# Transposes and gates of later tokens moved from the first attention steps into the opening maxima of a fused attention and mixture-of-experts block

## The chip, the core and the metric

The kernel runs on one core of a Trainium2 chip. The metric is device time in microseconds (us) of one execution; lower is better. The five queues that matter are named as in the profile: PE (TensorE, matrix products and transposes; PEld is its weight load), DVE (VectorE), ACT (ScalarE), POOL (GpSimd) and SP (SyncE, which issues most of the DMAs).

## What is computed

The input is x of shape 4 x 1024 x 256 (four sequences of 1024 tokens). All matrices are float32.

```python
xn = layernorm(x)                                   # over the 256 channels
x  = x + attention(xn) + moe(xn)
# attention: 16 heads of 16, rotary embedding, softmax(q k^T / 4) v, output projection
# moe: scores = sigmoid(xn @ w_gate.T), 16 experts in 4 groups, best 2 groups, best 4 experts,
#      routed SwiGLU experts (hidden 128) weighted by the scores, plus a shared SwiGLU (hidden 256)
```

## The kernel before

**Tokens.** There are 4096 tokens. The class `Norm` handles them in eight blocks of 512, numbered q = 0 to 7; blocks 2b and 2b+1 are sequence b. Four things are done to a block. `scale(q)` (L453) normalises it in place on ACT, four instructions of 128x256 with the factors `rstd` and `off`; these factors come from POOL (`power`, L371, L372, L409, L410 for blocks 2 to 4, L414, L416, L418 for 5 to 7). `turn(q, pair)` (L482, L486) transposes half a block: four transposes on PE into one bank of PSUM, and a copy by ACT into `part[q]`. `store(q)` writes the normalised rows to DRAM (`xnd`), and for blocks from 4 on the transposed part is written to `xnTd`. `gate(qs)` (L499, L508) multiplies the transposed parts with the gate weights, and `logits_of(qs)` (L515, L522) turns the products back and copies them to `logits`, from which the routing starts in step 9.

**Opening.** Blocks 0 and 1 (the first sequence) are normalised and turned first. A loop over ten values of t then makes q, k and v of sequence 0: products on PE (L1149), rotary embedding on DVE or POOL (`rotate`, L1180 to L1189), transposes back (`turn_unit`, L1216) and copies by ACT into `qT` and `kT` (L1221). The statistics of the later blocks run beside that, on DVE for blocks 2 to 4 and on ACT for 5 to 7 (L390, L396). In the same loop the first maxima are taken: `max_round(b, g, s)` makes four products `pm` (L1235), each 128x512, which DVE reduces to row maxima (L1243). A round with even s needs only the first half of `kT`, one with odd s the second half, and so the last copy of `kT`. After the loop come the factors of blocks 2 to 7 on POOL (issued after the last `rotate`), `scale(2)`, four rounds with odd s (16 products and 16 reductions), and `max_off` (L1254, L1258, L1263), which subtracts the maxima from q.

**Steps.** The attention then runs in 256 steps. A step makes four products `ps` (L1277) with four exponentials by ACT (L1286), four products `pm` with four maxima for the next head group, and four products `av` (L1302) of an earlier step's exponentials, whole (512 columns) or in two halves of 256. Steps 0 to 6 carry an additional round of maxima each (step 6 carries two). `moves(step)` issues scalings and stores, `pieces(step)` returns units that PE does in the middle of the step: turns, gates and logits of the blocks among them.

**What sets the order.** PE's instructions stay in the order of the text, and so do the copies of `turn_unit` for sequence 0, the statistics on ACT, the factors on POOL and `scale(q)` for q under 4. All other instructions are placed by the compiler's scheduler, which decides the order of each engine's queue by its own estimates; `issue_after` sets a lower bound for one group. All products share eight banks of PSUM in rotation, so a product waits until the reader of the bank eight places before it is done.

Of the kernel before, what the change touches and what calls it, by code (L numbers as in the profile page):

```python
# [20 lines left out]
NT = B * TT  # L21
# [7 lines left out]
HALF = 512  # L29
QT = 4  # L30
# [21 lines left out]
def kernel(  # L52
# [30 lines left out]
    k = Kit(tc, banks)  # L83
# [38 lines left out]
    norm = Norm(k, att, ff, keep, logits, power)  # L122
# [44 lines left out]
    with tc.issue_after(k.rotary):  # L167
        for power_of in powers:
            power_of()
    norm.scale(2)  # L170
    for qt in range(4):
        att.max_round(0, 0, 2 * qt + 1)
    att.max_off(0, 0, 0)

    def weights():
        nc.scalar.dma_start(out=k.w1s_sb, in_=w1s.rearrange("(c p) f -> p c f", p=P))
        nc.scalar.dma_start(out=k.w3s_sb, in_=w3s.rearrange("(c p) f -> p c f", p=P))
        nc.scalar.dma_start(out=k.w2s_sb, in_=w2s.rearrange("(c p) h -> p c h", p=P))
        k.sp(wout_sb, w_out.rearrange("(c p) f -> p c f", p=P))
# [81 lines left out]

    ex = ExitStack()
    now = pieces(0)
    for step in range(STEPS):
        beside.tick()
        norm.moves(step)
        if step in k.at_step:
            with tc.issue_after(k.last_exp):
                k.at_step[step]()

        bits = []
        if routing is not None and step >= ROUTE_FROM:
            bits += [advance] * (1 if step >= PUT_FROM else 2 if k.ranking else 3)
        if step >= PUT_FROM and beside.put_next < n_put:
            assert k.slots_known
            bits[:0] = [beside.put] * 2
        if step > done.get("tiles", STEPS):
            if beside.got == 0:
                ex.close()
                beside.rows = att.rows = ctx.enter_context(  # L280
                    tc.tile_pool(name="gp", bufs=4, side="right")
                )
            for _ in range(2 if step < STEPS - 2 * TT else 1):
                bits += [beside.get, beside.add]
        then = pieces(step + 1) if step + 1 < STEPS else []

        att.step(now, bool(then) and (step + 1 > 6 or step + 1 in norm.gates), bits)
        now = then
# [4 lines left out]
class Kit:  # L293


    def __init__(self, tc, banks):
        self.tc, self.nc, self.banks = tc, tc.nc, banks
        self.last_sp = self.last_exp = None
        self.ranking = self.slots_known = False
        self.summed = self.shared_rows = 0  # L300
# [26 lines left out]
class Norm:  # L327
# [3 lines left out]
    def __init__(self, k, att, ff, keep, logits, power):  # L331
        self.k, self.nc, self.att, self.ff = k, k.nc, att, ff
        self.logits, self.power = logits, power
        self.gates = {3: (2, 3, 4, 5), 5: (6, 7)}
        self.less = keep.tile([P, NT], F32, name="less")
        self.sq = keep.tile([P, NT], F32, name="sq")
        self.x4, self.xnT, self.part, self.lg = {}, {}, {}, {}
        self.mv, self.rstd, self.off, self.scaled = {}, {}, {}, None
# [28 lines left out]
    def power_of(self, q):  # L367
        nc, ff, mv = self.nc, self.ff, self.mv[q]
        rstd = self.rstd[q] = ff.tile([P, QT], F32, name=f"rstd_{q}", tag="rstd", bufs=8)
        keep = self.k.tc.keep_in_program_order  # L370
        keep(nc.gpsimd.tensor_scalar_add(mv[:, :, 1], mv[:, :, 1], 1e-5))  # L371
        keep(nc.gpsimd.tensor_tensor(rstd, mv[:, :, 1], self.power, ALU.pow))  # L372
# [155 lines left out]
    def moves(self, step):  # L528

        k = self.k  # L530
        q = step + 3
        if q < NT // QT:
            with k.tc.issue_after(k.last_exp or k.pace):
                self.scale(q)
        if step + 2 < NT // QT:
            self.store(step + 2)
        if 4 <= step + 1 < NT // QT:
            b, hf = divmod(step + 1, 2)
            k.sp(k.xnTd[b][:, :, hf * HALF : (hf + 1) * HALF], self.part[step + 1])

    def pieces(self, step, own):
        out = []
        if step + 2 < NT // QT:
            out += [lambda: self.turn(step + 2, 0), lambda: self.turn(step + 2, 1)]
        if own:
            out.append(own.pop(0))
        if step in self.gates:
            out.append(lambda: self.gate(self.gates[step]))
        if step - 1 in self.gates:
            out.append(lambda: self.logits_of(self.gates[step - 1]))  # L550
        return out + own
# [1002 lines left out]
```

## Time and profile before

| | |
|---|---|
| device time, median of 3 runs | 1416.7 us (1416.4 to 1418.83) |
| the profiled execution: device time | 1417.86 us |
| its span in the profile | 1416.2 us |
| PE, DVE, ACT, POOL busy | 98%, 66%, 55%, 30% of the span |
| mean granted PE clock | 0.993 |

The span is the time from the first to the last instruction that the profile shows; 1.66 us of the device time lie around it. The profiled execution took 1.16 us more than the median. PE's busy time is modelled from pipelined instructions, so a high share does not mean that it runs at its peak.

### The profile page before, as it was taken

The page shows a single profiled execution, that of the slowest core. Times are in us where ns is not written, and L with a number is a line of the kernel's source. Part 1 is how long each engine was busy: PE and PEld are TensorE (multiplying, and loading weights), DVE is VectorE, ACT ScalarE, POOL GpSimd, SP SyncE. Part 2 cuts the span into 40 slices and gives each one's busy share as a digit, 9 for nine tenths or more (in the row PEclk, how much of TensorE's full clock was granted, in tenths as well). Part 3 has the DMA queues.
Part 4 walks back from the last instruction along what each step waited for, and adds up shares of the span by engine and source line. Part 5 has one row for each costly group of instructions (what it writes and reads, how often), then busy time and mean ns, then how long its engine had stood idle before and what let it go on. Part 6 is the DMA issues. An engine that isn't in the chain of part 4 may idle for free.

```text
span 1416.2 us, 25822 instructions
## 1 busy us (share of the span) xinstructions
PE 1390.9 (98%) x9438; PEld 656.3 (46%) x9438; DVE 929.1 (66%) x1734; ACT 783.6 (55%) x1586; POOL 424.1 (30%) x498
## 2 busy tenths in 40 slices
PE   7899999999999999999999999999999999999998
PEld 4443233443343335666566665565664343333333
DVE  6879758678777765445554555554447988999941
ACT  4565445555555555556555555555555555555575
POOL 5401503764444464220000000002224444445400
PEclk9899999999999999999999999999999999999999
DMA  6134752424232314556666666665432434433310
GB/s 187 58 129 168 262 180 63 153 75 137 91 112 100 106 60 157 171 165 219 209 213 191 211 201 209 201 193 180 149 120 68 122 106 132 127 109 113 108 39 31
DMA packets 136670, 199.10 MB, mean 141 GB/s; under 512 B 13920, under 2 KB 99040, under 8 KB 136288
## 3 DMA queue, kind: packets, MB, share of 16 engines
q1 hardware_dynamic: 103088, 137.78, 30.6%
q0 software_dynamic: 12288, 33.57, 7.6%
q10 hardware_dynamic: 21168, 26.10, 5.4%
q8 instruction: 75, 1.23, 0.4%
q14 instruction: 51, 0.42, 0.1%
HBM read 124.01 MB, written 79.69 MB: 144 GB/s over the span
## 4 chain that ended last, share of the span: by engine, by line
PE 96%; DVE 2%; DMA 1%; ACT 1%; issue 0%; POOL 0%; ACTq 0%; POOLq 0%; DVEq 0%
PE ps L1277 20%; PE pm L1235 20%; PE av L1302 18%; PE ph_r L823 9%; PE exy L982 5%; PE ph_s L855 4%; PE pqk L1149 4%; PE py L1371 2%; PE pso L892 2%; PE pv L1149 2%; PE ext L973 2%; PE ptr L1216 2%; PE pmt L1258 1%; PE po L1326 1%; DVE mx L1243 1%; PE pt L482 1%
## 5 line engine op out<-in xcount | busy, mean ns | idle before, releaser
L1286 ACT ACTIVATE es<-ps 128x512 f32<-128x512 f32 x1024 | 554.8, 596 | 460.9 <-PE ps L1277 238.5
L1243 DVE TENSOR_REDUCE mx<-pm 128x1 f32<-128x512 f32 x1024 | 660.9, 685 | 188.4 <-PE pm L1235 138.5
L1277 PE MATMUL ps<-q,kT 32*128 32x512 f32 x1792 | 510.3, 643 | 4.2 <-DVE mx L1243 3.3
L1235 PE MATMUL pm<-kT,qT 32*128 32x512 f32 x1792 | 511.7, 643 | 1.4 <-ACT kT L1221 1.4
L1302 PE MATMUL av<-es,vv 128*32 128x512 f32 (+1 forms) x2136 | 277.4, 590 | 0.0
L1277 PEld LDWEIGHTS ps<-q,kT 32*128 32x128 f32 x1792 | 143.5, 183 | 193.7 <-ACT es L1286 140.0
L1235 PEld LDWEIGHTS pm<-kT,qT 32*128 32x128 f32 x1792 | 147.6, 183 | 64.7 <-DVE mx L1243 26.8
L831 DVE SCALAR_TENSOR_TENSOR th_r<-th_r,ph_r 128x256 f32<-128x256 f32 x72 | 30.3, 421 | 199.6 <-ACT th_r L830 199.6
L938 POOL DMA_INDIRECT xs<-rows,slot_i x128 | 124.0, 969 | 121.8 <-DVE mx L1243 107.7
L1030 POOL DMA_INDIRECT yg<-ys,slot_i x128 | 121.8, 951 | 119.1 <-DVE mx L1243 111.2
L1180 POOL TENSOR_TENSOR rot<-qk,sin_sb 128x256 f32<-128x256 f32 x56 | 39.5, 728 | 392.2 <-DVE qk L1137 392.0
L823 PE MATMUL ph_r<-xT,w 128*128 128x128 f32 x1152 | 140.5, 275 | 0.5 <-ACT xT L976 0.5
L1302 PEld LDWEIGHTS av<-es,vv 128*32 128x32 f32 x2136 | 42.9, 108 | 199.6 <-issue 177.7
L823 PEld LDWEIGHTS ph_r<-xT,w 128*128 128x128 f32 x1152 | 134.4, 192 | 0.8 <-ACT xT L976 0.7
L982 PE MATMUL exy<-w,gu_r 128*128 128x256 f32 x288 | 76.6, 388 | 0.0
L1277 PE MATMUL ps<-q,qkT 32*128 32x512 f32 x256 | 74.3, 640 | 0.0
L1235 PE MATMUL pm<-qkT,qkT 32*128 32x512 f32 x256 | 73.4, 640 | 0.0
L830 ACT ACTIVATE th_r<-ph_r 128x256 f32<-128x256 f32 x72 | 27.7, 384 | 82.6 <-PE ph_r L823 82.6
L982 PEld LDWEIGHTS exy<-w,gu_r 128*128 128x128 f32 x288 | 50.6, 190 | 28.9 <-issue 21.7
L1047 DVE SCALAR_TENSOR_TENSOR sum<-yg,wk,sum 128x256 f32<-128x256 f32 x128 | 63.7, 498 | 0.3 <-DMA yg<-ys,slot_i 0.3
L988 ACT ACTIVATE y<-exy 128x512 f32<-128x512 f32 x72 | 43.2, 600 | 35.0 <-PE exy L982 29.9
L1116 POOL MEMSET vv<- 128x128 f32 x4 | 1.3, 318 | 142.7 <-ACT es L1286 142.7
(178 smaller groups left out, 1230.0 us busy)
## 6 DMA issues: line engine op xcount, KB each, us to landing
w<-we SPq DMA_DIRECT2D x144, 384.0 KB, 4.0
xs<-zero ACTq DMA_DIRECT2D x8, 2304.0 KB, 8.1
xg<-xs SPq DMA_DIRECT2D x72, 256.0 KB, 4.7
ys<-y SPq DMA_DIRECT2D x72, 256.0 KB, 4.7
acc<-acc SPq DMA_DIRECT2D x14, 512.0 KB, 4.2
xb<-in_x_dram SPq DMA_DIRECT2D x16, 256.0 KB, 3.1
acc<-xb SPq DMA_DIRECT2D x16, 256.0 KB, 2.8
rows<-xnd SPq DMA_DIRECT2D x8, 512.0 KB, 5.8
```

The lines of the kernel that those rows point to most:

```text
L823: nc.tensor.matmul(ph[:, n, at], lhsT=w[n][:, c, :], rhs=xT[:, c, at], start=(c == 0), stop=(c == NC_ - 1),)
L855: nc.tensor.matmul(ph, lhsT=w[:, i, c * P : (c + 1) * P], rhs=self.xnT[b][:, i, at : at + SL], start=(i == 0), stop=(i == NC_ - 1),)
L938: put = nc.gpsimd.indirect_dma_start(out=k.xs, out_offset=bass.IndirectOffsetOnAxis(ap=k.slot_i[:, t, kk : kk + 1], axis=0), in_=self.rows ...
L982: nc.tensor.matmul(py[:, r, :], lhsT=gus[i][:, r * P : (r + 1) * P], rhs=got[i][1][:, r, 2 * NC_ * F :], start=True, stop=True,)
L1030: get = nc.gpsimd.indirect_dma_start(out=self.yg[:, kk, :], out_offset=None, in_=k.ys, in_offset=bass.IndirectOffsetOnAxis(ap=k.slot_i[:, ...
L1047: nc.vector.scalar_tensor_tensor(sm[:, 0, :], yg[:, kk, :], k.wk[:, t, kk : kk + 1], sm[:, 0, :], ALU.mult, ALU.add)
L1149: nc.tensor.matmul(ps, lhsT=self.xnT[b][:, c, t * P : (t + 1) * P], rhs=self.wqkv_sb[:, c, at : at + w], start=(c == 0), stop=(c == NC_ - 1),)
L1235: nc.tensor.matmul(ps, lhsT=self.qT[b, g // 2][rows, g % 2, qt * P : (qt + 1) * P], rhs=self.kT[b, g // 2][rows, g % 2, hf * HALF : (hf + ...
L1243: k.pace = nc.vector.tensor_reduce(out=self.mx_of[b, g, qt // 4][hf][:, qt % 4, j, :], in_=ps, axis=AX.X, op=ALU.max,).ins
L1277: nc.tensor.matmul(ps, lhsT=self.kT[b, g // 2][rows, g % 2, kc * P : (kc + 1) * P], rhs=self.q2[b, g, qh][rows, :], start=True, stop=True,)
L1286: k.last_exp = nc.scalar.activation(e, ps, AF.Exp, scale=DH**-0.5).ins
L1302: nc.tensor.matmul(av[32 * j : 32 * j + 32, cols], lhsT=self.vv[b][:, kc, h * VS : h * VS + 32], rhs=es[j][:, cols], start=(kc == 0), stop ...
```

## The change

Blocks 2 to 5 (the second and third sequence) are scaled and turned before step 0, between and after the four odd rounds of maxima, where before only block 2 was scaled. `scale(3)` follows `scale(2)`; the two turns of block 2 stand behind the second and third of these rounds, those of blocks 3 and 4 behind the fourth, those of block 5 behind `max_off`. `scale(4)` stands behind the second round, `scale(5)` ahead of `max_off`. In the steps, only blocks 6 and 7 are still scaled (in steps 0 and 1, before in steps 3 and 4) and turned (in steps 2 and 3, before 4 and 5). The gates of blocks 2 to 5 move from step 3 to step 1, those of 6 and 7 from step 5 to step 4; the logits follow a step later, as before. The writes of the transposed parts to `xnTd` are rearranged to fit. A step whose successor has a gate does its `av` product whole, so the steps that do this move as well.

```diff
@@ tile_block_kernel
     norm.scale(2)
+    norm.scale(3)
+
     for qt in range(4):
         att.max_round(0, 0, 2 * qt + 1)
+        if qt == 1:
+            norm.turn(2, 0)
+            norm.scale(4)
+        if qt == 2:
+            norm.turn(2, 1)
+    for q in (3, 4):
+        for pair in range(2):
+            norm.turn(q, pair)
+    norm.scale(5)
     att.max_off(0, 0, 0)
+    for pair in range(2):
+        norm.turn(5, pair)
@@ Norm.__init__
-        self.gates = {3: (2, 3, 4, 5), 5: (6, 7)}
+        self.turns, self.gates = {2: 6, 3: 7}, {1: (2, 3, 4, 5), 4: (6, 7)}
@@ Norm.moves
-        q = step + 3
+        q = step + 6
         if q < NT // QT:
             with k.tc.issue_after(k.last_exp or k.pace):
                 self.scale(q)
         if step + 2 < NT // QT:
             self.store(step + 2)
-        if 4 <= step + 1 < NT // QT:
-            b, hf = divmod(step + 1, 2)
-            k.sp(k.xnTd[b][:, :, hf * HALF : (hf + 1) * HALF], self.part[step + 1])
+        q = step + 4 if step < 2 else self.turns.get(step - 1)
+        if q:
+            b, hf = divmod(q, 2)
+            k.sp(k.xnTd[b][:, :, hf * HALF : (hf + 1) * HALF], self.part[q])
@@ Norm.pieces
-        if step + 2 < NT // QT:
-            out += [lambda: self.turn(step + 2, 0), lambda: self.turn(step + 2, 1)]
+        if step in self.turns:
+            out += [lambda i=i: self.turn(self.turns[step], i) for i in range(2)]
```

## Prediction

> **What bounds the kernel now.** The page says that the whole is a matter of PE: the chain that ended last lies on it for 96% of the span. That is an average, so I read next the same chain in order of time for the stretch that the change touches, from 43 us to 70 us.
>
> ```profile
> PE 96%; DVE 2%; DMA 1%; ACT 1%; issue 0%; POOL 0%; ACTq 0%; POOLq 0%; DVEq 0%
> ```
>
> ```profile
> 47.64 0.44 ACT kT L1221
> ...
> 48.12 1.18 PE pm L1235 x8
> 49.30 9.65 DVE mx L1243 x16
> ...
> 59.22 1.13 PE pmt L1258 x4
> ...
> 60.44 0.70 DVE q L1263
> ...
> 61.19 1.21 PE ps L1277
> ```
>
> (start, length, what.) The opening is a relay: ACT's last copy into kT lets the odd rounds start at 48.12, DVE then reduces 16 products in 9.65 us while PE has little to do, and the first product of step 0 comes at 61.19. Whoever delays that copy delays all of it. From 61.19 on the chain is PE's, with each turn as a link (`PE pt`, 1.66 us in step 0, 1.02 to 1.03 us in steps 1 to 5).
>
> The second view is the timeline, of ACT and then of POOL, just before these rounds.
>
> ```profile
> 45.09 0.64 ACT L1221 COPY qT<-ptr 128x256 f32<-128x256 f32 x2
> ...
> 47.64 0.70 ACT L1221 COPY kT<-ptr 128x256 f32<-128x256 f32 x2
> 48.17 4.14 ACT L453 ACTIVATE qkT<-qkT,off,rstd 128x256 f32<-128x256 f32 x8
> ```
>
> ```profile
> 47.26 0.23 POOL L410 TENSOR_SCALAR off<-off 128x4 f32<-128x4 f32 x1
> ...
> 49.97 0.23 POOL L410 TENSOR_SCALAR off<-off 128x4 f32<-128x4 f32 x1
> ...
> 52.51 0.24 POOL L410 TENSOR_SCALAR off<-off 128x4 f32<-128x4 f32 x1
> ...
> 54.46 0.20 POOL L418 TENSOR_TENSOR off<-less,rstd 128x4 f32<-128x4 f32 x1
> ```
>
> ACT scales only after its last copy, at 48.17. POOL finishes the factors of blocks 2, 3, 4 and 5 at 47.49, 50.20, 52.75 and 54.66, one behind the other, with no gap that something could fill.
>
> The third view is the busy time by stage: steps 0 to 6, cut at each step's first `ps`.
>
> ```profile
> 61.20:67.90 6.70, 6.70 (x35) 3.48 (x36) 3.16 (x6) 3.21 (x7) 0.00 (x0) 0.75 0.00 0
> 67.90:74.60 6.70, 6.70 (x39) 2.81 (x37) 5.80 (x11) 5.45 (x12) 0.00 (x0) 1.00 0.63 196
> ...
> 103.00:110.90 7.90, 7.90 (x59) 3.31 (x55) 7.47 (x15) 2.86 (x6) 0.00 (x0) 1.00 0.02 9
> ```
>
> (Window, length, busy PE, PEld, DVE, ACT, POOL, granted PE clock, DMA.) Step 6, with twelve maxima and no turn, keeps DVE busy 7.47 of 7.90 us, while steps 0 to 5, with eight maxima, last 6.4 to 7.65 us.
>
> **Part 1: the turns leave the steps.** Blocks 2 to 5 are four turns of eight transposes. Of the six steps with a turn, four lose theirs: 1.66 us (the one in step 0, at a clock of about half) and 3 x 1.03 us, 4.75 us of links on the path. Is there room? A step without turn would be 6.4 - 1.03 = 5.4 us, above its eight reductions (8 x 0.61 = 4.9 us), so DVE does not take the gain away at once. Three scalings (2.06 us of ACT each, blocks 4 to 6) leave the steps too; they delay exponentials (the first of step 2 starts at 76.20, as the scaling from 74.24 ends), but no link of the chain is ACT's there. I take 0, bounds 0 and 1.0 us. One more `av` is split, two halves of 0.57 us for one whole of 1.00: +0.14. The gates and logits cost PE the same in their new steps. Sum -4.6 us, bounds -6.0 (scalings count, step 0 gets the full clock) and -3.0 (DVE's idle pieces around its eight reductions come back in part).
>
> **Part 2: the turns in the opening.** The transposes of blocks 2 to 4 stand among 16 products that DVE takes 0.60 us each to reduce; six groups of four (1.03 / 2, or 1.66 / 2 at half clock) are 3.1 to 5 us beside 9.65 us. The banks suffice: a turn's bank is wanted again eight allocations later, some 4.8 us of reductions. I cost them at 0; if the cover were gone, it is those 3.1 to 5 us. Block 5 is different: its eight transposes stand between `pmt` and the first `ps`. Before, `pmt` to `ps` is 1.97 us (59.22 to 61.19), at a clock of half. PE now needs 1.12 + 1.73 = 2.85 us there at half clock (+0.88), or 0.66 (the `pmt` at 112.43) + 1.09 = 1.75 us at full, when DVE's part is also shorter (-0.4). I take +0.4 and keep both ends.
>
> **Part 3: what the moved scalings do to ACT's queue.** This decides the sign. `scale(4)` and `scale(5)` are not held in the order of the text, and the order of the changed program's instructions on ACT shows where the scheduler put them:
>
> ```
> ... 6 squares of blocks 6 and 7 (L396)
> scale(4) x2                     waits for off of block 4 (POOL)
> qT, qT, kT, kT of token tile 6
> 2 squares of block 7
> scale(4) x2, scale(5) x3        waits for off of block 5 (POOL)
> qT, qT, kT, kT of token tile 7  <- the copy that the odd rounds need
> scale(2) x4, scale(3) x4, scale(5) x1, scale(6) x4, then the copies of the turns
> ```
>
> Up to the first of these lines all queues stand as before, and POOL's whole order is unchanged. So ACT comes to `scale(4)` at 45.09, where it copied qT before, and the factors come at 52.75: a wait of 7.66 us. Queued behind it are the eight copies of tiles 6 and 7, for which PE waits, and for PE DVE. To this come seven scalings ahead of the last kT copy, at 4.14 / 8 = 0.52 us each: 3.6 us. The odd rounds start at 48.12 + 11.3 = 59.4 instead of 48.12. `off` of block 5 (54.66) is there before ACT gets to it (about 56.9). POOL does not wait for anything behind the stall before block 7's factors, so there is no second stall.
>
> [...]
>
> Then the clock. PE has no instruction from 46.75 to 59.4. Before, the granted clock was 0.50 from 54.65 to about 64.8, after a stretch with thinly spread products. So I start the rounds at half clock: the first reduction came 1.16 us after its product at 48.12, but 2.15 us after the one at 61.19, at half: +1.0 us (bounds +0.2 and +1.0). Sixteen reductions at 0.60 us are slower than PE at either clock.
>
> [...]
>
> **The sum.** Stall and scalings +11.3, cold first products +1.0, block 5 ahead of `ps` +0.4: step 0 begins at about 73.9 instead of 61.19. Steps -4.6. Together +8.1 us. Nothing after step 6 is changed, and PE bounds it, so the delay stays. The profiled execution (span 1416.2, 1.66 around it) becomes 1417.86 + 8.1 = 1426.0; the median of the runs lies 1.16 us below that execution, so I say 1424.8. Bounds: 11.0 + 0.2 - 0.4 - 6.0 = +4.8 (1421.5) and 11.6 + 1.0 + 0.9 - 3.0 = +10.5 (1427.2).
>
> **Rivals.** (1) The turns' gain does not come: DVE paces steps 0 to 5 at what they cost now, and the steps give back 1 us only. For it: DVE is busy 5.80 of 6.70 us in step 1. Against: in step 2 it idles 1.08 us exactly during the turn. Then +11.7, 1428.4; chance 0.12. (2) The change does what its text says: ACT isn't held up. That needs block 4's `off` ready at 45.1 rather than 52.75, or copies that run past the waiting scaling. Then -4.6, with part 2 hidden: 1412.1. It decides from the point where stall and scalings together are under about 3 us. Against it: POOL's rotation ends only at 45.15, and the factors follow it in order. Chance 0.06. (3) The delay is made up: scalings and half clock were dearer in the steps than I count, and 8 to 10 us come back. Then within 0.2%: 1418; chance 0.05. My forecast keeps 0.77.
>
> About 0.2% (2.8 us) is what a measurement of this kernel can tell from no change. Slower by more: 0.77 + 0.12 = 0.89; within: 0.05; faster: 0.06. The range, 1421.0 to 1428.5, takes in the bounds and rival 1.
>
> **What would show it.** In the changed profile ACT should idle some 7.7 us before its first L453, released by POOL; the odd `pm` should start near 59.4, `pmt` near 71.5, the first `ps` near 73.9; steps 0 to 6 should take about 45 us instead of 49.7. I am wrong if ACT shows no such wait, if `pm` starts before 55, or if the steps are not shorter.

## The result and the profile after

The changed kernel takes 1420.9 us (median of 12 runs, 1419.68 to 1422.58) against 1416.89 us for the kernel before (12 runs, 1415.1 to 1419.21): ratio 1.0027, 95% interval 1.0019 to 1.0034, or 2.7 to 4.8 us slower. The forecast was 1424.8 us with a range from 1421.0 to 1428.5: the sign was right, the size (+8.1 us) was twice what was measured (+4.0), and the median lies 0.1 us below the range.

The chain of waits of the profile after (start, length, what) has a new beginning: it no longer comes to the odd maxima by ACT's copies alone but by POOL's factors.

```profile
52.14 0.25 POOL off L424
...
52.41 1.09 ACT qkT L467 x2
...
55.56 2.45 ACT qkT L467 x5
...
58.53 0.28 ACT kT L1236
...
58.85 2.12 PE pm L1250 x8
60.98 9.65 DVE mx L1258 x16
...
70.90 0.66 PE pmt L1273 x4
71.55 0.87 PE pt L496 x8
72.43 0.67 PE ps L1292
```

(Line numbers are larger by 14 or 15 than before.) The odd products start at 58.85 instead of 48.12. The timeline of ACT and of PE gives the two waits, in square brackets (the idle time before the row, and what ended it):

```profile
52.41 1.09 ACT L467 ACTIVATE qkT<-qkT,off,rstd 128x256 f32<-128x256 f32 x2 [7.51 <-POOL off L424]
58.85 3.79 PE L1250 MATMUL pm<-kT,qT 32*128 32x512 f32 x16 [12.41 <-ACT kT L1236]
```

ACT idles 7.51 us for block 4's factor, and PE, whose kT copy stands behind it, 12.41 us. The busy time by stage, of steps 0, 1 and 6 (columns as in the prediction):

```profile
72.40:76.70 4.30, 4.30 (x29) 2.45 (x28) 3.10 (x6) 2.98 (x7) 0.00 (x0) 1.00 1.01 322
76.70:83.60 6.90, 6.90 (x50) 2.16 (x48) 6.36 (x11) 4.59 (x9) 0.00 (x0) 1.00 0.87 288
...
108.30:115.90 7.60, 7.60 (x55) 3.38 (x51) 7.17 (x14) 2.95 (x6) 0.00 (x0) 1.00 0.00 1
sum 43.50, PE 43.50 PEld 18.00 DVE 36.56 ACT 21.40 POOL 0.95; mean PE 6.21 PEld 2.57 DVE 5.22 ACT 3.06 POOL 0.14
```

Steps 0 to 6 take 43.5 us instead of 49.7; step 0 shrank most, from 6.70 to 4.30 us, and its granted clock is 1.00 instead of 0.75. The cut between steps 0 and 1 lies at the second product `ps` of step 1, about 1.1 us late, here and in the profile before, where the prediction calls it the first; from first product to first product step 0 went from 5.58 to 3.14 us, which is the same 2.4 us less.

In what follows four places serve as marks: the start of the odd products, the first reduction of them, the first `ps`, and the `pmt` of step 7. Between the two profiles the change has cost 5.0 us at that `pmt` (117.46 against 112.43), but only 2.6 us at the end of the span (1418.8 against 1416.2). Where the rest went is a question for the experiments.

### The profile page after: what moved, and what is told of

The parts are those of the page before. It is cut to its first block, busy times and chain, and to the rows that moved or that the text cites. A ratio compares the mean times of both kernels' runs of the same rounds, so it can differ in the third digit from the quotient of the medians.

```text
span 1418.8 us, 25831 instructions
## 1 busy us (share of the span) xinstructions
PE 1385.4 (98%) x9446; PEld 655.4 (46%) x9446; DVE 929.6 (66%) x1734; ACT 784.3 (55%) x1586; POOL 424.4 (30%) x498
## 4 chain that ended last, share of the span: by engine, by line
PE 95%; DVE 2%; POOL 1%; DMA 1%; ACT 1%; issue 0%; ACTq 0%; POOLq 0%; DVEq 0%
PE ps L1292 20%; PE pm L1250 20%; PE av L1317 18%; PE ph_r L838 9%; PE exy L997 5%; PE ph_s L870 4%; PE pqk L1164 4%; PE py L1386 2%; PE pso L907 2%; PE ext L988 2%; PE pv L1164 2%; PE ptr L1231 2%; PE pmt L1273 1%; PE po L1341 1%; DVE mx L1258 1%; PE pf L1374 1%
```

## The experiments

Ratios are to the kernel before on the same chip and in the same session, with 95% intervals. The places come from each kernel's one profile, in us; starting points differ by up to 1 us between profiles of the same kernel, so the differences in the second and third column say more than the first.

| kernel | odd products start | first reduction to first `ps` | first `ps` to `pmt` of step 7 | ratio |
|---|---|---|---|---|
| before | 48.12 | 11.91 | 51.24 | |
| before_again | 49.11 | 11.89 | 51.65 | |
| changed | 58.85 | 11.44 | 45.06 | 1.0027 (1.0019 to 1.0034) |
| after_again | 59.03 | 11.44 | 45.04 | 1.0043 (1.0029 to 1.0057) |
| order_kept | 48.46 | 11.70 | 45.05 | 0.9959 (0.9943 to 0.9975) |
| scalings_only | 59.91 | 11.90 | 51.03 | 1.0060 (1.0047 to 1.0073) |
| scalings_kept | 48.72 | 11.90 | 50.12 | 0.9989 (0.9979 to 0.9998) |
| dose | 61.42 | 11.70 | 45.05 | 1.0039 (1.0024 to 1.0053) |
| gates_late | 48.04 | 11.70 | 45.31 | 0.9954 (0.9940 to 0.9967) |
| six_too | 48.56 | 11.69 | 45.05 | 0.9946 (0.9932 to 0.9959) |
| filler | 49.42 | 11.44 | 49.65 | 0.9986 (0.9975 to 0.9997) |

**order_kept: the change without the stall.** The scheduler may no longer place the scalings of blocks 4 to 6 ahead of the last copies into kT.

```diff
 # Norm.scale, changed kernel
-            if q < 4:
+            if q < 7:
                 self.k.tc.keep_in_program_order(scale)
```

> The changed kernel, but the scalings of blocks 4, 5 and 6 are held in the order of the text, so that none of them stands ahead of the last copies into kT. Theory A (ScalarE's wait for the factors of block 4 and seven scalings ahead of the last copy cost the opening some 11 us; the turns taken out of the steps bring about 6 us): the odd maxima start near 48.1 us again, the first ps near 61 us, and steps 0 to 6 stay as short as in the changed kernel (45.1 us from the first ps to the pmt of step 7): pmt near 106.5 us, device time 5 to 7 us under the kernel before, about 1411. Rival B (the turns themselves hold up the opening, since PE and the banks are not free beside the maxima): first ps not before 64 us, device time at or above that of the kernel before.

The odd products start at 48.46, the first `ps` at 61.32, `pmt` at 106.37, and the kernel is 3.6 to 8.1 us faster than before (0.25% to 0.57% of 1423.63 us in that session). Theory A is right in every place, and rival B is out: with the transposes among the odd maxima, first reduction to first `ps` is 11.70 us against 11.91, so they cost the opening nothing. The chain that leads to its first exponential runs over the products and turns, and at its end over ACT's scaling of block 6, which led to six_too below:

```profile
48.46 2.00 PE pm L1250 x16
50.46 0.59 PE pt L496 x4
51.04 2.83 PE pm L1250 x8
53.87 0.59 PE pt L496 x4
54.46 1.80 PE pm L1250 x8
...
62.01 0.57 ACT x L467 x2
...
63.98 0.49 ACT es L1301
```

**scalings_only: the stall without the turns.** The kernel before with the scalings in their new places.

```diff
 # kernel before
     norm.scale(2)
+    norm.scale(3)
     for qt in range(4):
         att.max_round(0, 0, 2 * qt + 1)
+        if qt == 1:
+            norm.scale(4)
+    norm.scale(5)
     att.max_off(0, 0, 0)
 # Norm.moves
-        q = step + 3
+        q = step + 6
```

> The kernel before, with only the scalings moved as in the change (blocks 3, 4 and 5 ahead of step 0, block 6 in step 0, block 7 in step 1); turns, gates and writes stay in their old steps. Theory A: the stall of the changed kernel is here too (odd maxima near 58.9 us, first ps near 72.4 to 73), but not the gain: steps 0 to 6 take about 49 to 51 us to the pmt of step 7 as before, and device time is 10 to 12 us above the kernel before (1427 to 1429). Rival C (the 6 us gained in the steps come from the scalings that left them, not from the turns): steps as short as in the changed kernel, about 45 us, and device time about 4 to 5 us above the kernel before.

The stall is there (ACT idles 7.52 us, odd products at 59.91) and the steps stay at 51.03 us. So theory A holds for both places, and rival C, by which all the gain comes from the scalings, is out. That a part of it does come from them, the next kernel shows; in scalings_only TensorE was at half clock (0.50) from 73.9 to 79.0, over 5 us of step 0 where it was 3.4 us in the kernel before (0.50 from 61.2 to 64.6), which hides some of what the scalings gave back. The device time rose less than expected, 6.7 to 10.4 us instead of 10 to 12. The profiled execution, 1434.21 us, was the longest of five (median 1431.4); where the rest went is not shown.

**scalings_kept: the scalings moved, without stall.** This is scalings_only with `q < 7` in the condition of order_kept.

> As scalings_only, with the scalings of blocks 4, 5 and 6 held in the order of the text, behind the last copies into kT: no stall. Theory A: the opening is as before (odd maxima near 48.1 us, first ps near 61.2), the steps too, device time within 1.5 us of the kernel before. Rival C (the scalings made the steps long): pmt of step 7 near 107 us rather than 112, device time about 5 us under the kernel before.

It is 0.3 to 3.0 us faster, and the steps are 1.1 us shorter than the first profile of before (50.12 against 51.24; 1.5 against the second). Theory A's "as before" is a little off: scalings in the steps were not quite free.

**dose: another wait, other work.** This is the changed kernel with `q < 6` in that condition, so block 6's scalings are placed early instead of block 4's.

> The changed kernel with the scalings of blocks 4 and 5 held in the order of the text, but not that of block 6: the scheduler then puts two scalings of block 6 where two of block 4 stood, and two more ahead of the copies of token tile 7, so that ScalarE waits for factors that come about 3.7 us later, with four scalings ahead of the last copy instead of seven. Theory A: ScalarE idles about 11.2 us instead of 7.5 and the odd maxima start near 61.0 us, 2.2 us later than in the changed kernel; device time about 2 us above it (1423). A theory in which the place of the scalings matters by the work they add (rival D): start near 57.3 us, 1.5 us earlier, and 1419.

```profile
56.44 1.09 ACT L467 ACTIVATE x<-x,off,rstd 128x256 f32<-128x256 f32 x2 [11.03 <-POOL off L432]
```

ACT idles 11.03 us and the odd products start at 61.42, 2.57 us later than in the changed kernel (0.5 us of it because this profile is later as a whole: POOL's factors began at 45.44 instead of 44.94). Four scalings instead of seven stand ahead of the copy, and it is still later: rival D, by which the added work alone decides, is out. Both count: the wait is 3.5 us longer, the three scalings fewer save about 1.5. Device time, 3.4 to 7.5 us above before, fits theory A but is too wide to show 2 us.

**gates_late: of the turns and gates, only the turns of blocks 2 to 5 moved.**

```diff
 # Norm.__init__, on top of order_kept
-        self.turns, self.gates = {2: 6, 3: 7}, {1: (2, 3, 4, 5), 4: (6, 7)}
+        self.turns, self.gates = {4: 6, 5: 7}, {3: (2, 3, 4, 5), 5: (6, 7)}
```

> As order_kept (the change without the stall), but the turns of blocks 6 and 7 and all gates stay in the steps of the kernel before (turns in 4 and 5, gates in 3 and 5): only the turns of blocks 2 to 5 are moved. Theory A: the sooner gates bring nothing, since the routing starts in step 9 in any case: first ps to the pmt of step 7 within 0.5 us of order_kept's 45.05 us, device time within 2 us of order_kept. Rival E (sooner gates are worth something): 1 us or more longer to the pmt, or a longer stretch behind it.

It takes 45.31 us in the steps against 45.05, and its ratio is order_kept's, as far as two intervals of some 4 us width from two sessions can tell. The sooner gates bring nothing that these runs can measure.

**six_too: block 6 scaled in the opening too.**

```diff
 # on top of order_kept
     norm.scale(5)
+    norm.scale(6)
     att.max_off(0, 0, 0)
 # Norm.moves
-        if q < NT // QT:
+        if step and q < NT // QT:
```

> As order_kept, but block 6 is scaled with block 5 ahead of the last maximum instead of between the last turns and the first exponentials (all scalings held in the order of the text, block 7 in step 1). Theory A: the first exponential of step 0 starts about 2 us sooner than in order_kept (63.98 us there); since the maxima on VectorE pace step 0, this brings 0 to 1 us, device time 0 to 1 us under order_kept and 6 to 8 us under the kernel before. A rival in which the exponentials pace step 0: 2 us under order_kept.

It is 5.8 to 9.7 us faster than before (0.9932 to 0.9959 of 1420.79 us), but its 45.05 us to the `pmt` are order_kept's. What it was made for did not come: the first exponential starts at 63.79 instead of 63.89, not 2 us sooner. In both kernels ACT is busy without a gap from block 5's scaling (58.90 and 58.80) to that exponential, with block 6's scaling and the two copies of block 5's last turns in between; only the order of these two changed. So this run does not decide whether the exponentials pace step 0, and whether it is better than order_kept the two intervals don't tell.

**filler: the clock alone.** Twenty-four transposes that nobody reads, at the places of the moved turns of blocks 2 to 4.

```diff
 # kernel before
+    def filler(n):
+        pt = k.bank([P, 4, P], f"fill_{n}")
+        for i in range(4):
+            k.pe(nc.tensor.transpose(pt[:, i, :], k.ident, k.ident))
+
     for qt in range(4):
         att.max_round(0, 0, 2 * qt + 1)
+        if qt in (1, 2):
+            filler(qt)
+    for n in range(4):
+        filler(4 + n)
     att.max_off(0, 0, 0)
```

> The kernel before, with 24 additional transposes of the identity at the places where the changed kernel has those of blocks 2 to 4 (four behind the second and third odd round, sixteen behind the fourth); nobody reads them, and nothing else is moved. Theory A (the transposes among the odd maxima keep TensorE's clock open, whatever they are good for, and that is part of the gain): no half clock between 50 and 66 us; first reduction of the odd rounds to first ps about 11.5 us instead of 11.9, first ps to the pmt of step 7 about 50.3 us instead of 51.2 to 51.65 (step 0 no longer cold); device time 1 to 1.5 us under the kernel before. Rival F (the clock closes because the rounds are thin, and 24 transposes do not change that, so that in the changed kernel the clock opened for another reason): half clock at 55 to 65 us as before, 11.9 and 51.2 us, device time unchanged.

Busy time and granted clock (the number before the last two) of the odd maxima, first of the kernel before, then of filler:

```profile
49.28:54.65 5.37, 5.37 (x23) 2.49 (x19) 5.37 (x9) 3.03 (x7) 4.99 (x31) 0.97 0.55 183
54.65:61.19 6.54, 2.68 (x8) 0.72 (x5) 5.17 (x10) 0.00 (x0) 2.81 (x7) 0.50 0.17 52
```

```profile
50.58:54.65 4.07, 4.07 (x20) 1.60 (x14) 4.07 (x7) 3.02 (x7) 3.69 (x29) 1.00 0.40 138
54.65:62.00 7.35, 5.13 (x33) 3.31 (x32) 6.46 (x12) 0.00 (x0) 4.08 (x10) 1.00 0.35 104
```

The clock stays at 1.00 where it was 0.50. First reduction to first `ps` falls to 11.44 us, as in the changed kernel, the steps to 49.65 (50.3 was expected), and the kernel gets faster by 0.4 to 3.6 us for work that is of no use. Theory A is right and rival F is out: the transposes among the odd maxima hold the clock open, and that is a gain of its own, some 0.5 us in the opening and 1.6 us in step 0 (2.0 against the second profile of before).

**after_again and before_again: the stretch behind step 7.** Both kernels unchanged, for a second profile.

> The changed kernel unchanged, for a second profile and beside the other kernels on one chip. Theory A (everything behind step 7 costs the same in both kernels, apart from how long TensorE's clock happens to be halved between 130 and 220 us): 3 to 6 us above the kernel before; odd maxima near 58.9, first ps near 72.4, pmt of step 7 near 117.5 us; the stretch from the first to the third reciprocal of the attention (81.3 us in the first profile) between 80.5 and 84.5 us, longer with more time at half clock. Rival E (the sooner gates shorten that stretch for good): again 81.3 us or less, and the kernel before again 84.5.

> The kernel before unchanged, for a second profile. Theory A: first to pmt of step 7 as in the first profile (first ps to that pmt 51.2 us), but the stretch from the first to the third reciprocal of the attention between 81 and 84.5 us with less than 10.2 us at half clock. Rival E: 84.5 us again.

The changed kernel is 4.1 to 8.1 us slower than before here (3 to 6 were expected). From the `pmt` of step 7 to the first reciprocal of the attention (L1331 before) it is 19.25 or 19.26 us in all eleven profiles, whatever the kernel. From there to the third reciprocal the length differs, and for the most part it goes with the clock. The rows of this stretch in the first profiles of before and changed, then in the second ones:

```profile
131.70:216.20 84.50, 81.20 (x467) 29.49 (x468) 57.69 (x107) 39.04 (x73) 23.40 (x33) 0.94 0.60 214
```

```profile
136.70:218.00 81.30, 78.42 (x468) 29.48 (x468) 57.77 (x108) 39.07 (x73) 23.37 (x33) 0.98 0.63 223
```

```profile
133.07:214.70 81.63, 79.20 (x468) 29.15 (x468) 55.98 (x108) 39.04 (x73) 24.05 (x33) 0.96 0.62 222
```

```profile
136.88:219.60 82.72, 79.38 (x468) 29.25 (x468) 57.67 (x107) 39.03 (x73) 23.38 (x33) 0.96 0.61 219
```

A mean of 0.94, 0.96 and 0.98 means about 10, 6.5 and 3.3 us at half clock (an estimate: the share that is missing, twice, by the length; the clock records of the first profiles of before and changed hold 1.00 and 0.50 only, with 10.2 and 3.4 us at 0.50 in these rows). Over all eleven profiles the stretch took 80.7 and 81.3 us at 0.98, 81.6 to 83.4 us at 0.96 (seven profiles), and 84.5 and 84.6 us at 0.94; the 1.9 us within the middle group are not explained by it. The kernel before was once in the longest group and once in the middle one; six_too, a fast kernel, was in the longest. Rival E, 3 us for good from the sooner gates, is out: the stretch varies by that much from run to run of one kernel. A small effect is not: the five profiles with the sooner gates average 82.2 us, the six others 83.0, and each set spreads over 3 to 4 us. The first pair of profiles happened to draw 3.3 us in favour of the changed kernel, and 0.9 us came back behind the third reciprocal; this is how 5.0 us at step 7 became 2.6 us at the end. In the second pair 3.81 us at the `pmt` (117.62 against 113.81) became 3.3 us at the end. What sets which group a run falls into stays open.

## Why the prediction was right and wrong

The sign and its mechanism were right; two terms of the sum were mis-sized, block 5 ahead of the first `ps` and the steps. The step of the prediction behind the first and part of the second is the clock, taken over from the kernel before, where it was 0.50 from 54.65 on into step 0; behind another part of the second it is "I take 0" for the scalings.

**The stall: right.** This decided the sign, as said. Predicted 7.66 us of wait and seven scalings, a start at 59.4; measured 7.51 us and 58.85, of which 0.3 us is POOL starting sooner in this profile. order_kept takes it away by one condition, scalings_only brings it back without any turn, dose lengthens it with less work. That no copy runs past a scaling that waits, which the 7.66 us rest on, no row of before showed; here it was so: in the changed kernel PE's transposes for the eight copies end at 46.44, and the first of the copies starts at 53.41, behind the scaling.

**Cold first products: right.** From the first odd product to the first reduction it is 2.11 us instead of 1.16, +0.95 (predicted +1.0), at a granted clock of 0.50 (58.85 to 63.40) instead of 1.00 (46.00 to 49.28).

**Block 5 ahead of the first `ps`: wrong side.** I took +0.4 from bounds of -0.4 and +0.9. Measured: `pmt` to `ps` 1.50 us instead of 1.97, so -0.47, just past the end for an open clock. The step that failed is the clock of half, carried over from before, where `pmt` to `ps` lay at 0.50. The clock opened during the odd maxima of the changed kernel and stayed open to the first `ps` (number before the last two):

```profile
58.85:63.70 4.85, 4.84 (x23) 2.08 (x26) 2.74 (x5) 4.85 (x11) 0.00 (x0) 0.53 0.32 108
63.70:72.40 8.70, 7.31 (x48) 4.73 (x48) 7.79 (x14) 5.16 (x11) 0.00 (x0) 1.00 0.10 36
```

I had transferred a row of thin rounds without transposes to rounds with twenty-four of them. The same stall without them, in scalings_only, reads:

```profile
65.00:70.00 5.00, 3.07 (x14) 1.54 (x9) 5.00 (x10) 1.51 (x4) 0.00 (x0) 0.84 1.03 334
70.00:73.90 3.90, 1.11 (x4) 0.71 (x4) 2.55 (x5) 0.00 (x0) 0.00 (x0) 0.50 0.13 45
```

The 0.84 is an estimated 3.4 us at 1.00 within the 5 us, the rest at 0.50, so here it opened too, with the products alone, but it fell again and the first `ps` (73.91) came at half clock. So the transposes are not shown to open the clock; that they keep it open, filler shows (1.00 where it was 0.50). The clock opened 4.6 us after the first odd product in the changed kernel, and 5.1 to 6.7 us after it in scalings_only (0.50 up to 65.0, and 3.4 us open before 70.0).

**The steps: right mechanism, too small.** Predicted -4.6 us with the scalings at 0; measured -6.2 (45.06 against 51.24), just past the bound of -6.0 that was to hold both the scalings and an open clock in step 0. filler shows 1.6 us of the 6.2 as step 0's open clock, of which my term for the first turn held 0.63. scalings_kept shows another 1.1 us for the scalings, which I had put at 0, though with the bound of 1.0 beside it. If the three add up, which no run shows, the four turns themselves are some 3.5 us of the path, where I had 4 x 1.03. The places in the chain where a turn stood as a link were a fair guide; DVE did not take the gain away, so rival 1 did not come. The counted half of `av` cannot be told apart in these sums.

**Behind step 7: right as far as it can be seen.** "The delay stays" holds from the `pmt` to the first reciprocal to 0.01 us. The next 85 us vary by some 4 us between profiles, which one profile of before cannot show; in the first pair they favoured the changed kernel by 3.3 us, in the second the kernel before by 1.1 us.

The sum by the measured terms at the `pmt` of step 7 is 10.73 + 0.95 - 0.47 - 6.18 = +5.0, where I had 11.3 + 1.0 + 0.4 - 4.6 = +8.1. Nearly all of the miss, 2.5 of 3.1 us, is in the two terms that depend on the clock and on the scalings; where the last 1 us to the medians' +4.0 lies is not shown. With the second profiles the same sum is 9.92 + 0.95 - 0.45 - 6.61 = +3.8, because before_again starts its odd products 1 us later, so the first pair alone is good to about 1 us. **Rival 2**, that the change does what its text says, became true only once the order was held: there it gave 3.6 to 8.1 us, around the 4.6 that I had put on it, but with the open clock and the scalings in it, most of which the 4.6 had left out.

## What to carry to other kernels

A step moved forward in the text is moved in every queue, and where a scheduler places it by its own estimates, an instruction that waits for a slow engine can land ahead of work that everyone else needs (here ACT waited 7.51 us for POOL with the last copies into kT behind it); compare the order of each queue, and hold it by hand where it matters. Read the granted clock as a term of its own: in this kernel, work that filled a thin stretch also paid by keeping the clock open behind it (1.00 instead of 0.50 in filler, some 0.5 us in the opening and 1.6 us in step 0). Before a difference of 3 us in one pair of profiles is explained, look whether the same kernel shows it against itself.

## What was not expected of the hardware

PE's row was busy for all of 5.37 us (49.28 to 54.65, before) and the clock still fell to 0.50 (the 0.97 of that row is its last 0.3 us, so it fell a little ahead of the 54.65 that the prediction gives); with twenty-four full 128x128 transposes between the same products it stayed at 1.00 (filler). So the busy time of this row, which is modelled, does not say whether the clock stays open. What lets it fall no run here shows.

The three sessions of the experiments, each on another chip, gave the unchanged kernel before 1423.63, 1420.79 and 1421.04 us, against 1416.89 beside the changed kernel. In the second profile of before 349.7 us lie behind the 21st reciprocal, in the first 344.0; nothing of the change stands there. The changed kernel's first profile has 344.9, and all nine profiles of the experiments lie between 348.1 and 349.9, whatever the kernel, so this goes with the session. All ratios above are therefore within one session; the places of the profiles, and gates_late and six_too against order_kept, are compared across sessions.
